# Two-layer sequence model on one core: the third token block of the feed-forward layer is turned by transfers and VectorE, and its products move past the first branches of the recurrence

## The chip, the cores and the metric

The kernel runs on one core of a Trainium2 chip. The metric is the device time of one execution in microseconds (us); the time of a kernel is the median of its runs. TensorE (PE) multiplies matrices into PSUM; VectorE (DVE), ScalarE (ACT) and GpSimd (POOL) work on tiles; SyncE (SP) issues most transfers. Every engine runs its own instructions in a fixed order and waits on semaphores for the others.

## The reference

The input is 2 x 1024 tokens of 512 floats. Two layers follow each other; each adds an attention-like part and a feed-forward part to its input and normalizes the sum over the 512 features:

```python
x = _layernorm(x + _L0_attn_ref(x, ...))   # state-space block
x = _layernorm(x + _L0_ffn_ref(x, ...))    # one linear layer, then a rescaling of each token's row
x = _layernorm(x + _L1_attn_ref(x, ...))   # gated linear recurrence
x = _layernorm(x + _L1_ffn_ref(x, ...))    # silu(x Wg) * (x Wu), then Wd
```

The two in the middle are what the change touches:

```python
# _L0_ffn_ref
out = jnp.einsum('bln,nk->blk', x, weight) * scale      # weight is -1, 0 or 1, 512 x 512
# ... out is scaled by a function of its row's norm
# _L1_attn_ref
y = gelu(x @ w_y + b_y)
xb = x @ w_x + b_x
conv = causal convolution of xb over 4 tokens
gate_x, gate_a = sigmoid(conv @ w_ig + b_ig), sigmoid(conv @ w_ag + b_ag)
h_t = a_t * h_{t-1} + x_t                                # along the tokens
out = (h * y) @ w_out + b_out
```

## The kernel before, in words

The 2048 tokens are four blocks of 512 (`NBLK`, numbered 0 to 3). A block in "row" form has tokens on the partitions (`X[b]`, four groups of 128 tokens, j = 0 to 3); a product needs it "turned", with features on the partitions (four groups of 128 features, k = 0 to 3).

The kernel has two ways to turn a block. `transposed` lets TensorE multiply by an identity, 16 products of 128 x 128, and ScalarE and VectorE take the results from PSUM. `load_blocks` and `turn_blocks` need the rows in device memory: four transfers read them so that 32 x 32 pieces come to the right place, and VectorE turns the pieces in four instructions, one for each k.

`linear(b)` is the feed-forward part of the first layer for one block. It is a generator that the code around it advances from `yield` to `yield`. Its first step turns the block and cuts it into two pieces of reduced precision: ScalarE casts the value to the high piece (tile `wu`) and VectorE subtracts that from the value for the low piece (tile `wd`). The next two steps are the products, two token groups each (`po`, 8 matmuls for a group, high and low piece by turns), each followed on VectorE by a multiplication from PSUM (`o`) and on ScalarE by a sum of squares. The last step rescales the rows, adds them to `X[b]`, normalizes (for blocks 1 to 3 the four passes of the normalization run on GpSimd), and stores the block to `x_lin`. The tiles of the two pieces have one buffer: block b+1 can be cast only when the products of block b are done.

`branches(b)` starts the recurrence for a block: four products with `w_x` (m = 0 to 3), each taken out of PSUM by ScalarE into `xpad`, a tile of two buffers with three pad columns in front, and convolved by VectorE in four instructions (one scaled copy into `cv`, three taps); then four products with `w_y`, each through GELU on ScalarE. For block 0 the pad columns are zeroed by GpSimd. `gates(b)` multiplies the convolved block by `w_ig` and `w_ag`; `project_back(b)` multiplies by `w_out` at the end.

`weave(main, fill, plan)` walks through `main` and advances `fill` by `plan[i]` steps after step i; what is left of `fill` is run at the end. A scheduler then chooses each engine's order from the program's order and its own estimates; `tc.keep_in_program_order` and `tc.high_priority` bind or raise single instructions.

Around the change the order is this. `linear(0)` and `linear(1)` run among the last products of the first layer's attention part. Then `branches(0)` is woven with `linear(2)` by the plan `(1,) * 4`: block 2 is turned by TensorE right after block 0, and its products stand between those of `w_x`. Block 3 was read in pieces (`mid`, by `load_blocks` from `x_mid`, the output of the attention part), VectorE turns it, and its products stand between those of `gates(0)`. The weights `w_out` take the buffer of the turned block 0 (tag `w4`); they are asked for in `linear(3)`.

Of the kernel before, what the change touches and what calls it, by code (L numbers as in the profile page):

```python
# [9 lines left out]
F32 = mybir.dt.float32  # L10
# [6 lines left out]
P = 128  # L17
TB = 512
NJ = TB // P
D = 512  # L20
NK = D // P
# [16 lines left out]
def model_kernel(ctx: ExitStack, tc: tile.TileContext, t: dict, out: bass.AP):  # L38
    nc = tc.nc
    ctx.enter_context(nc.allow_non_contiguous_dma(reason="small parameter columns"))  # L40
    BATCH, SEQ, _ = t["L0_attn_hidden_states"].shape
    NBLK = BATCH * SEQ // TB
# [3 lines left out]
    x_mid = tc.dram_tile([NBLK, TB, D], F32, name="x_mid")  # L46
# [35 lines left out]
    X = [tokens() for _ in range(3)]  # L82
# [49 lines left out]
    w_out = op.tile([P, NX, D], F32, tag="w_out", name="w_out")  # L132
# [90 lines left out]
        nc.vector.tensor_scalar(r, z, 0.0, None, ALU.max)  # L223
        nc.vector.scalar_tensor_tensor(o, p, 2.0, r, ALU.mult, ALU.add)

    def transposed(pool, b, X, tags=("xT",), split=False, bufs=1, by_act=False, behind=False, soon=False):


        pieces = [
            pool.tile([P, NK, TB], F32R if split else F32, tag=tag, name=f"{tag}{b}", bufs=bufs)  # L230
            for tag in tags
        ]
        xT = pieces[0]
        for k in range(NK):
            pt = bank("pt")
            for j in range(NJ):
                nc.tensor.transpose(  # L237
                    pt[:, j * P : (j + 1) * P], X[b][:, j, k * P : (k + 1) * P], ident
                )
            if split:  # L240
                copied = nc.scalar.copy(xT[:, k, :], pt)
                if behind:
                    tc.keep_in_program_order(copied)
                nc.vector.tensor_tensor(
                    pieces[1][:, k, :], pt, xT[:, k, :].bitcast(F32), ALU.subtract
                )
            elif soon:
                with tc.high_priority():
                    nc.scalar.copy(xT[:, k, :], pt)
            elif k % 2 or by_act:  # L250
                nc.scalar.copy(xT[:, k, :], pt)
            else:
                nc.vector.tensor_copy(xT[:, k, :], pt)
        return pieces
# [6 lines left out]
    def load_blocks(dst, rows, pinned=False):  # L261

        blocks = rows.rearrange("(n t) (k a c) -> a t k n c", t=32, k=NK, c=32)
        for a in range(4):
            load = nc.sync.dma_start(
                dst[32 * a : 32 * a + 32].rearrange("t k (n c) -> t k n c", c=32), blocks[a]
            )
            if pinned:
                tc.keep_in_program_order(load)

    def turn_blocks(dst, src=None, pinned=False):
        for k in range(NK):
            turned = nc.vector.transpose(dst[:, k, :], (src or dst)[:, k, :])
            if pinned:
                tc.keep_in_program_order(turned)
# [28 lines left out]
    def weave(main, fill, plan, rest=True):  # L304

        for i, _ in enumerate(main):
            for _ in range(plan[i] if i < len(plan) else 0):
                next(fill, None)
        for _ in fill if rest else ():
            pass  # L310
# [561 lines left out]
    def later_layers(exact, last=None):  # L872
# [65 lines left out]
        def split(x, pieces):  # L938


            for k in range(NK):
                nc.scalar.copy(pieces[0][:, k, :], x[:, k, :])
                if exact:
                    nc.vector.tensor_tensor(
                        pieces[1][:, k, :], x[:, k, :], pieces[0][:, k, :].bitcast(F32),
                        ALU.subtract,
                    )
# [7 lines left out]
        def linear(b):  # L955

            tags = ("wu0", "wd0") if exact else ("wu0",)
            if b == NBLK - 1:
                turn_blocks(mid)
                w1.append(wp.tile([P, NK, D], F32, tag="w4", name="w14" + suffix))  # L960
                xT = [ep.tile([P, NK, TB], WT, tag=tag, name=f"{tag}{b}") for tag in tags]
                split(mid, xT)
                nc.sync.dma_start(w1[4], w_sources["w_out"])
            else:

                xT = transposed(ep, b, X, tags=tags, split=exact, behind=b == 2)
            yield
            o = ep.tile([P, NJ, D], F32, tag="wF", name="o" + suffix)
            ssq = sp.tile([P, NJ], F32, tag="ssq", name="ssq")
            for j in range(NJ):  # L970
                po = bank("po")
                for k in range(NK):
                    for x in xT:
                        nc.tensor.matmul(  # L974
                            po, x[:, k, j * P : (j + 1) * P], wf[:, k, :],
                            start=(k == 0 and x is xT[0]), stop=(k == NK - 1 and x is xT[-1]),
                        )
                nc.vector.tensor_tensor(o[:, j, :], po, f0s, ALU.mult)
                junk = ep.tile([P, GW], mybir.dt.bfloat16, tag="junk", name="junk2")
                nc.scalar.activation(junk, o[:, j, :], AF.Square, accum_out=ssq[:, j : j + 1])  # L980
                if j % 2:
                    yield
            norm = sp.tile([P, NJ], F32, tag="norm", name="norm")
            nc.scalar.activation(norm, ssq, AF.Sqrt)
            v = sp.tile([P, NJ], F32, tag="v", name="v")
            nc.vector.tensor_scalar(v, norm, 1e-7, None, ALU.max)
            f = sp.tile([P, NJ], F32, tag="f", name="f")
            nc.scalar.activation(f, v, AF.Tanh)
            nc.vector.tensor_scalar(v, v, 1e-7, None, ALU.add)
            nc.vector.reciprocal(v, v)  # L990
            nc.vector.tensor_tensor(f, f, v, ALU.mult)
            nc.vector.tensor_tensor(norm, norm, f, ALU.mult)
            nc.vector.tensor_scalar(norm, norm, 1e-7, None, ALU.max)
            nc.vector.reciprocal(norm, norm)
            nc.vector.tensor_scalar(norm, norm, 0.99, 1.0, ALU.mult, ALU.min)
            nc.vector.tensor_tensor(f, f, norm, ALU.mult)
            for j in range(NJ):
                nc.vector.scalar_tensor_tensor(
                    X[b][:, j, :], o[:, j, :], f[:, j : j + 1], X[b][:, j, :],
                    ALU.mult, ALU.add,  # L1000
                )
            layernorm(X[b], engine=nc.gpsimd, last=None if b else nc.vector)
            if b:
                store_rows(x_lin[b], X[b])
            yield
# [39 lines left out]
        with tc.tile_pool(name="rec" + suffix, bufs=1, side="right", reuse_waits="tile") as rp:  # L1045
            carry = rp.tile([P, NK, 3], F32, tag="carry", name="carry1")
            last_h = rp.tile([P, NK], F32, tag="last", name="last")

            mid = rp.tile([P, NK, TB], F32, tag="xT", name="mid" + suffix)
            load_blocks(mid, x_mid[3])  # L1050
            nc.sync.dma_start(X[3], rows_mid[3])

            def product(i, m, rhs):
# [8 lines left out]
            def branches(b, st):  # L1062

                if b:
                    xT = rp.tile([P, NK, TB], F32, tag="xT", name=f"xT{b}")
                    turn_blocks(xT, lin.pop(0))
                    if b + 1 < NBLK:
                        lin.append(coming_block(b + 1))
                else:

                    xT = transposed(wp, b, X, tags=("w4",), by_act=True, soon=True)[0]
                yield
                cv = st["cv"] = rp.tile([P, NK, TB], F32, tag="cv", name="cv", bufs=2)
                y = st["y"] = rp.tile([P, NK, TB], F32, tag="y", name="y", bufs=2)
                for m in range(NK):
                    pm = product(0, m, xT)
                    xpad = rp.tile([P, 3 + TB], F32, tag="xpad", name="xpad1", bufs=2)
                    if b % BPS == 0:
                        nc.gpsimd.memset(xpad[:, 0:3], 0.0)
                    else:  # L1080
                        nc.gpsimd.tensor_copy(xpad[:, 0:3], carry[:, m, :])
                    nc.scalar.activation(xpad[:, 3:], pm, AF.Identity, bias=bx[:, m : m + 1])
                    if b % BPS < BPS - 1:
                        nc.gpsimd.tensor_copy(carry[:, m, :], xpad[:, TB : TB + 3])
                    nc.vector.tensor_scalar(
                        cv[:, m, :], xpad[:, 3:], cw1[:, m, 3:4], cb1[:, m : m + 1],
                        ALU.mult, ALU.add,
                    )
                    causal_conv(cv[:, m, :], xpad, cw1[:, m, :])
                    yield  # L1090
                for m in range(NK):
                    pm = product(1, m, xT)
                    nc.scalar.activation(y[:, m, :], pm, AF.Gelu, bias=by[:, m : m + 1])
                    yield
# [76 lines left out]
                yield  # L1171

            st = {}
            weave(branches(0, st), linear(2), (1,) * 4)
            lin = [coming_block(1)]
            bout = row("L1_attn_b_out", D, c1, nc.sync, "scale")
            ys = []
# [256 lines left out]
```

## Time and profile before

| what | value |
|---|---|
| median of 3 runs | 1119.91 us (1119.85 to 1121.25) |
| the profiled execution's own time | 1119.75 us |
| its span in the profile | 1118.0 us |
| TensorE busy | 1099.4 us, 98% of the span |
| VectorE busy | 704.4 us, 63% |
| ScalarE busy | 452.7 us, 40% |
| GpSimd busy | 364.5 us, 33% |

The profile is of one execution; 1.75 us of its own time lie around the span. Lines such as L237 are lines of the kernel before. A matmul of plain 32-bit floats has two records in the profile, one of the reduced 32-bit type (`fp32r`, used by `linear`) and a transposition by TensorE have one. Durations of neighbouring records overlap, so a pace is read from the starts.

### The profile page before, as it was taken

What the parts mean: (1) busy time and instruction counts of PE and PEld (TensorE: products, weight loads), DVE (VectorE), ACT (ScalarE), POOL (GpSimd) and SP (SyncE); (2) the same over time, 40 slices, a digit from 0 to 9 for tenths busy, and PEclk for the clock granted to TensorE, in tenths of its full rate; (3) what the DMA queues carried; (4) which work ended last, traced back from release to release, by engine and by line L of the source; (5) the groups of instructions that cost most, each with busy time, mean ns of one, the idle gap of its engine ahead of it and who ended that gap; (6) DMA issues with size and microseconds to landing.
All of it is one profiled execution on the core that took longest, in us unless ns stands there. A gap on an engine that the chain in (4) does not pass through costs nothing.

```text
span 1118.0 us, 12076 instructions
## 1 busy us (share of the span) xinstructions
PE 1099.4 (98%) x4450; PEld 663.6 (59%) x4450; DVE 704.4 (63%) x1267; ACT 452.7 (40%) x692; POOL 364.5 (33%) x346
## 2 busy tenths in 40 slices
PE   9999999999999999999999999999999999999996
PEld 5455445445544555745444444447888888888885
DVE  5989797697869676874647438184238865325224
ACT  3334633463454233466654372553233224224223
POOL 1546471465248340273533231236411001001000
PEclk9999999999999999999999999999999999999998
DMA  8004202801220138336550001204654002100001
GB/s 323 21 9 122 94 1 92 207 0 38 88 98 0 39 124 226 67 94 153 111 76 25 13 1 44 32 0 138 192 95 76 1 1 62 15 1 32 6 1 41
DMA packets 122059, 77.04 MB, mean 69 GB/s; under 512 B 94512, under 2 KB 95312, under 8 KB 120456
## 3 DMA queue, kind: packets, MB, share of 16 engines
q1 hardware_dynamic: 120792, 75.77, 25.6%
q8 instruction: 37, 0.61, 0.2%
q10 hardware_dynamic: 976, 0.39, 0.1%
q14 instruction: 30, 0.25, 0.1%
q0 software_dynamic: 224, 0.02, 0.0%
HBM read 59.95 MB, written 16.02 MB: 68 GB/s over the span
## 4 chain that ended last, share of the span: by engine, by line
PE 81%; DVE 11%; ACT 4%; issue 1%; POOL 1%; DMA 1%; SPq 0%; DVEq 0%; ACTq 0%; POOLq 0%
PE pgu L1026 20%; PE p L1056 19%; PE po L1257 10%; PE pg L372 9%; PE px L372 7%; PE po L770 4%; DVE acc L298 3%; PE po L1146 2%; PE py L705 2%; PE po L974 2%; DVE L L578 2%; PE pxt L674 1%; PE pt L237 1%; DVE st L283 1%; POOL x L1152 1%
## 5 line engine op out<-in xcount | busy, mean ns | idle before, releaser
L1037 DVE SCALAR_TENSOR_TENSOR h<-pgu,L_ffn_up_scale,sg 128x512 f32<-128x512 f32 x63 | 47.1, 748 | 126.6 <-PE pgu L1026 122.8
L770 PE MATMUL po<-w_out,xc 128*128 128x512 f32 x256 | 112.5, 593 | 2.8 <-DVE L L578 2.8
L372 PE MATMUL px<-xT,w_in 128*128 128x512 f32 x256 | 114.6, 597 | 0.0
L593 POOL TENSOR_TENSOR L<-L,gm 128x512 f32<-128x512 f32 x64 | 93.4, 1490 | 64.8 <-DVE bdec L588 38.3
L372 PE MATMUL pg<-xT,w_in 128*128 128x512 f32 x256 | 113.5, 594 | 0.0
L1056 PE MATMUL p<-cv,w 128*128 128x512 f32 x256 | 110.8, 592 | 0.0
L1026 PE MATMUL pgu<-wF__4239,wg 128*128 128x512 f32 x256 | 101.7, 397 | 0.0
L1026 PE MATMUL pgu<-lo__4240,wg 128*128 128x512 f32 x256 | 100.8, 394 | 0.0
L1026 PE MATMUL pgu<-lo__4240,wu 128*128 128x512 f32 x256 | 100.7, 393 | 0.0
L1026 PE MATMUL pgu<-wF__4239,wu 128*128 128x512 f32 x256 | 100.7, 393 | 0.0
L1257 PE MATMUL po<-wd,hh 128*128 128x512 f32 x252 | 98.2, 396 | 0.3 <-POOL wg L917 0.3
L1257 PE MATMUL po<-wd,hl 128*128 128x512 f32 x252 | 98.2, 396 | 0.2 <-DVE hl L1041 0.2
L1036 ACT ACTIVATE sg<-pgu,L_ffn_gate_scale 128x512 f32<-128x512 f32 x63 | 43.4, 688 | 127.7 <-PE pgu L1026 127.6
L770 PEld LDWEIGHTS po<-w_out,xc 128*128 128x128 f32 x256 | 48.4, 190 | 63.8 <-issue 56.2
L1040 ACT CAST hh<-h 128x512 fp32r<-128x512 f32 x63 | 39.1, 620 | 112.5 <-DVE h L1037 112.3
L1056 PEld LDWEIGHTS p<-cv,w 128*128 128x128 f32 x256 | 48.6, 190 | 60.4 <-issue 59.1
L1056 PE MATMUL p<-xT,w 128*128 128x512 f32 x192 | 82.9, 592 | 0.0
L372 PEld LDWEIGHTS px<-xT,w_in 128*128 128x128 f32 x256 | 47.5, 190 | 57.5 <-issue 56.0
L372 PEld LDWEIGHTS pg<-xT,w_in 128*128 128x128 f32 x256 | 47.3, 190 | 54.2 <-issue 53.3
L1375 POOL TENSOR_TENSOR x<-x,r 128x512 f32<-128x512 f32 x12 | 15.1, 1291 | 195.2 <-DVE r L1374 195.2
L298 DVE SCALAR_TENSOR_TENSOR acc<-xpad,cols,acc 128x512 f32<-128x512 f32 x72 | 67.0, 933 | 18.5 <-ACT acc L342 13.8
L578 DVE TENSOR_TENSOR_SCAN L<-pl,id 128x512 f32<-128x512 f32 x64 | 74.9, 1205 | 4.5 <-ACT pl L572 3.5
(294 smaller groups left out, 1926.1 us busy)
## 6 DMA issues: line engine op xcount, KB each, us to landing
L<-decays SPq DMA_DIRECT2D x12, 1024.0 KB, 7.3
x_mid<-x SPq DMA_DIRECT2D x4, 1024.0 KB, 4.3
x<-x_mid SPq DMA_DIRECT2D x4, 1024.0 KB, 7.9
st<-in_L_ffn_gate_w_dram SPq DMA_DIRECT2D x8, 512.0 KB, 5.8
st<-in_L_ffn_up_w_dram SPq DMA_DIRECT2D x8, 512.0 KB, 4.1
st<-in_L_ffn_down_w_dram SPq DMA_DIRECT2D x8, 512.0 KB, 3.7
x_rec<-x SPq DMA_DIRECT2D x4, 1024.0 KB, 4.7
x<-_attn_hidden_states_dram SPq DMA_DIRECT2D x3, 1024.0 KB
```

Of the source, the lines that this page charges most:

```text
L298: tap = nc.vector.scalar_tensor_tensor(acc, xpad[:, k : k + TB], w[:, k : k + 1], acc, ALU.mult, ALU.add)
L372: nc.tensor.matmul(pm[:n, :], w_in[:, k, lo : lo + n], xT[:, k, :], start=(k == 0), stop=(k == NK - 1),)
L578: nc.vector.tensor_tensor_scan(L[:, h, :], pl, id4.rearrange("p j t -> p (j t)"), 0.0, ALU.mult, ALU.add)
L593: nc.gpsimd.tensor_tensor(L[:, h, :], L[:, h, :], st["gm"], ALU.mult)
L705: nc.tensor.matmul(pys[i][hh * HD : (hh + 1) * HD, q, :], dtx[q][:, 2 * i + hh, :], L[:, h, s], start=(first and q == 0), stop=(q == 1), s ...
L770: nc.tensor.matmul(po, xc[:, m, j * P : (j + 1) * P], w_out[:, m, :], start=(m == 0), stop=(m == NX - 1),)
L1026: nc.tensor.matmul(pm, w[g][:, k, cols], x[:, k, :], start=(k == 0 and x is pieces[0]), stop=(k == NK - 1 and x is pieces[-1]),)
L1036: nc.scalar.activation(sg, pgu[0], AF.Silu, scale=gs[:, m : m + 1])
L1037: nc.vector.scalar_tensor_tensor(h, pgu[1], us[:, m : m + 1], sg, ALU.mult, ALU.mult)
L1040: nc.scalar.copy(halves[0], h)
L1056: nc.tensor.matmul(pm, w1[i][:, k, m * P : (m + 1) * P], rhs[:, k, :], start=(k == 0), stop=(k == NK - 1),)
L1257: nc.tensor.matmul(po[j], x[:, j * P : (j + 1) * P], wd[m // GK][:, m % GK, :], start=(m == 0 and x is h[0]), stop=(m == NF - 1 and x is h ...
```

## The change

Block 2 is now read in pieces and turned by VectorE as block 3 was. Both tiles are allocated at the start of the recurrence's pool, block 2 in one of the two buffers of `y`, and their eight transfers are issued with raised priority. The plan of the weave becomes `(0, 0, 0, 0, 1, 0, 1, 1)`: block 2 is turned and cut after the four products of `w_x`, its first two product groups come after the second product of `w_y`, the other two after the third, and its last step after `branches(0)`. The load of `w_out` moves from `linear(3)` to the end of that weave. The argument `behind` of `transposed`, which bound block 2's copies, goes.

```diff
-    def transposed(pool, b, X, tags=("xT",), split=False, bufs=1, by_act=False, behind=False, soon=False):
+    def transposed(pool, b, X, tags=("xT",), split=False, bufs=1, by_act=False, soon=False):
...
             if split:
-                copied = nc.scalar.copy(xT[:, k, :], pt)
-                if behind:
-                    tc.keep_in_program_order(copied)
+                nc.scalar.copy(xT[:, k, :], pt)
...
-            if b == NBLK - 1:
-                turn_blocks(mid)
-                w1.append(wp.tile([P, NK, D], F32, tag="w4", name="w14" + suffix))
+            if b > 1:
+                turn_blocks(mid[b])
                 xT = [ep.tile([P, NK, TB], WT, tag=tag, name=f"{tag}{b}") for tag in tags]
-                split(mid, xT)
-                nc.sync.dma_start(w1[4], w_sources["w_out"])
+                split(mid[b], xT)
             else:
-
-                xT = transposed(ep, b, X, tags=tags, split=exact, behind=b == 2)
+                xT = transposed(ep, b, X, tags=tags, split=exact)
...
-            mid = rp.tile([P, NK, TB], F32, tag="xT", name="mid" + suffix)
-            load_blocks(mid, x_mid[3])
+            mid = {}
+            for b, tag, bufs in ((2, "y", 2), (3, "xT", 1)):
+                mid[b] = rp.tile([P, NK, TB], F32, tag=tag, name=f"mid{b}{suffix}", bufs=bufs)
+                with tc.high_priority():
+                    load_blocks(mid[b], x_mid[b])
             nc.sync.dma_start(X[3], rows_mid[3])
...
-            weave(branches(0, st), linear(2), (1,) * 4)
+            weave(branches(0, st), linear(2), (0, 0, 0, 0, 1, 0, 1, 1))
+            w1.append(wp.tile([P, NK, D], F32, tag="w4", name="w14" + suffix))
+            nc.sync.dma_start(w1[4], w_sources["w_out"])
```

## The prediction

> **What bounds the kernel now.** I read the page's busy times first, then its chain, then the chain and each engine's timeline between 440 and 530 us, where the change lies, and last the busy times by stage at the end of the span for the clock.
>
> ```profile
> PE 1099.4 (98%) x4450; PEld 663.6 (59%) x4450; DVE 704.4 (63%) x1267; ACT 452.7 (40%) x692; POOL 364.5 (33%) x346
> PE 81%; DVE 11%; ACT 4%; issue 1%; POOL 1%; DMA 1%; SPq 0%; DVEq 0%; ACTq 0%; POOLq 0%
> ```
>
> TensorE is never far from busy: 18.6 us of 1118.0 are idle. So a change is worth the TensorE work that it takes away, less every new pause of TensorE. The chain through the stage shows that there is no pause now:
>
> ```profile
> 458.43 3.49 PE pt L237 x32
> 461.92 3.44 PE p L1056 x8
> 465.36 3.67 PE po L974 x16
> 469.03 3.43 PE p L1056 x8
> 472.46 3.64 PE po L974 x16
> 476.11 27.47 PE p L1056 x64
> ```
>
> Columns are start, length, engine and line. First come the 32 transpositions (16 of block 0, 16 of block 2), then w_x and block 2's products by turns, then w_x, w_y and the first gate products. Paces: a transposition 3.49/32 = 0.109 us; a record of p 27.47/64 = 0.429 us, so a product of four matmuls (8 records) 3.43 us; a matmul of linear 3.64/16 = 0.228 us.
>
> **What goes.** Sixteen transpositions on TensorE: 16 x 0.109 = 1.75 us, all of it on the path. That is the whole possible gain, 0.16% of the time, less than the 0.2% that a measurement of this kernel can tell from no change.
>
> **What moves on TensorE.** In the changed kernel's order of instructions TensorE runs block 0's 16 transpositions, then six products without a break (four of w_x, two of w_y), and then needs block 2's pieces. It gets there at 458.43 + 1.75 + 6 x 3.43 = 480.8 us. Nothing independent stands behind: only one matmul of w_y is put between the first of block 2's.
>
> **When the pieces are there.** On VectorE the order puts all convolutions of block 0 first, then the four turnings of block 3, then the four of block 2, then block 2's four subtractions. (Block 3's stand first although they are needed later.) The last convolution is the one that waits, for GpSimd. These are GpSimd's and VectorE's timelines of before, and one cast of ScalarE:
>
> ```profile
> 475.36 0.10 POOL L1079 MEMSET xpad<- 128x3 f32 x1 [1.40 <-DVE cv L298]
> 476.08 8.95 POOL L291 TENSOR_SCALAR x<-x,mv,rs 128x512 f32<-128x512 f32 x4 [0.62 <-DVE rs L289]
> 484.98 0.10 POOL L1079 MEMSET xpad<- 128x3 f32 x1
> ```
> ```profile
> 475.75 0.17 DVE L289 RECIPROCAL rs<-rs 128x4 f32<-128x4 f32 x1
> 490.74 0.72 DVE L298 SCALAR_TENSOR_TENSOR cv<-xpad,cw,cv 128x512 f32<-128x512 f32 x1
> 491.50 1.54 DVE L298 SCALAR_TENSOR_TENSOR cv<-xpad,cw,cv 128x512 f32<-128x512 f32 x2
> 493.04 2.46 DVE L273 STREAM_TRANSPOSE mid<-mid 128x512 f32<-128x512 f32 x4
> 495.42 0.68 DVE L944 TENSOR_TENSOR wd<-mid,wu 128x512 fp32r<-128x512 f32 x1
> ```
> ```profile
> 493.75 0.62 ACT L942 CAST wu<-mid 128x512 fp32r<-128x512 f32 x1 [1.58 <-DVE mid L273]
> ```
>
> The fourth xpad's pad columns are zeroed (484.98) behind the four normalization passes of block 1, since GpSimd keeps its order; that order is the same after the change, and the first tap reads those columns. Before, this cost nothing: VectorE was late itself (first tap 490.74) and TensorE asked for the convolved block only after 496. Now TensorE's next products stand behind it. Step by step:
>
> - Start of the passes. VectorE loses four subtractions of block 2 (L244) and two multiplications (L978) ahead of it, and its first convolution starts about 2 us earlier, because TensorE delivers w_x's first product at 460.2 + 3.4 = 463.6 instead of 465.4. But one tap more (0.67) comes before the last statistics, and ScalarE takes out the third product (0.6) before the table load and the square root. I put the passes at 475.3 instead of 476.1; bounds 474.8 and 476.1.
> - Their length. Block 1's four took 8.95 us, beside a VectorE that was busy throughout; block 3's took 8.24 at 530.08. VectorE will be idle for the second half, so 8.7. Pads zeroed at 484.1 (bounds 483.1 to 485.1).
> - Three taps: from 490.74 to 492.95 with an aggregate between them, so 2.1. Done at 486.2.
> - Block 3's four turnings: 495.42 - 493.04 = 2.38, done at 488.6. Block 2's first cast can start 0.71 after its first turning (493.75 - 493.04) and takes 0.62; with 0.1 for the semaphore TensorE resumes at 490.0.
> - The subtractions wait for all eight turnings: 486.2 + 4.76 = 491.0, then four at 0.62 give 493.5. The last matmul of the first token group ends at 493.7.
>
> From 480.8 to 493.7 TensorE has nine matmuls of linear (2.05 us) and one of w_y (0.86): 2.9 us of work in 12.9. The pause is 10.0 us, and from there on TensorE has everything.
>
> **The clock.** A pause this long has a second price. At the end of the span the last matmul is over by 1109; these are the busy times by stage, with the granted clock third from the end:
>
> ```profile
> 1108.00:1110.00 2.00, 0.88 (x4) 0.38 (x2) 1.93 (x6) 1.62 (x5) 1.28 (x2) 1.00 0.28 93
> 1110.00:1112.00 2.00, 0.00 (x0) 0.00 (x0) 1.58 (x4) 1.94 (x6) 0.13 (x1) 0.88 0.46 166
> 1112.00:1114.00 2.00, 0.00 (x0) 0.00 (x0) 0.71 (x2) 0.14 (x1) 0.00 (x0) 0.50 0.52 186
> ```
>
> After some 2.6 us without matmuls the clock is 0.50. How long it stays there once work is back, no row shows directly; the nearest is the span's start, where 24 records of 128 x 128 (L188) take 4.92 us, 0.205 each, twice the 0.107 that 0.429 for 512 columns would make. Bounds: nothing, or 4.92 us at half speed from 490.0. In the second case 2.46 us of the 2.9 are done at 494.9, and the group ends at 495.35 instead of 493.7, 1.65 us lost. I take the middle, 0.85.
>
> [...]
>
> **What costs nothing, and its cover.** SP issues eight loads of 256 KB (1.15 us each by its timeline: 3 in 3.45) instead of four, from 462 on, all ahead of block 1's store to x_lin, which waits for GpSimd until 484 anyway. Before, three were in by about 470; eight are in by 480 at the latest, six us before the turning at 486. Without that cover each us late is a us lost. The load of w_out now waits for the last w_y product, at about 505, on SP's queue; the last quarter of block 1's lin load (needed after 515) stands behind it. It lands some 7 us after its issue, so at 512; cover 3 us and more. VectorE gains four turnings (2.4 us) and loses nothing else; it sits in the pause. Block 3's casts wait for block 2's last product, now 3.43 + 2 x 3.43 = 10.3 us ahead of block 3's first product (27 us before). Behind four casts (2.2), a table load (1.28) and a sum of squares (0.8) that is enough.
>
> **Sum.** -1.75 + 10.0 + 0.85 = +9.1 us on the profiled 1119.75, so 1128.9; the median of the runs stands 0.16 above that execution: 1129.0.
>
> **Rivals.**
> - Faster: the pieces are ready before TensorE asks, and only the 16 transpositions go: 1119.9 - 1.75 = 1118.2. It needs VectorE to begin the eight turnings by 473.5 (480.8 less 7.3 for turnings and subtractions). Against it stands the order: at 475.75 VectorE was still at block 1's statistics. Three chances in 100.
> - GpSimd isn't in the way (the tap does not wait for the zeroed pads). Then VectorE's own work counts: the fourth convolution starts about 478.5, done 480.6, last subtraction 487.9, pause 488.1 - 480.8 - 2.9 = 4.4. With 0.5 for the clock: +3.2, 1123.1. For it: the row 476.08 names only rs as its releaser. Against: taps read the pad columns. Eight in 100.
> - A second pause: block 3's pieces come late as well, the 10.3 us being too few for ScalarE's queue of casts, table loads and GELUs. Two to four us more: 1132.0. For it: block 1's pieces were 0.8 us late at 451.74 in the same form. Seven in 100.
>
> **How the numbers follow.** The forecast has 82 in 100. Its own bounds: pads 483.1 to 485.1 (-1.0, +1.0) and the clock 0 to 1.65 (-0.85, +0.8) give 1127.1 to 1130.8. I stretch that to 1126.0 and 1132.0, which takes in most of the second pause and leaves out the other two rivals. Faster by over 0.2% (under 1117.7): 0.02, the first rival's far end. Same: 0.02. Slower: 0.96.
>
> **What would show it.** Right: TensorE's records stop near 481 and resume near 490, at the first po of L974, with a granted clock of 0.50 there; block 2's turnings on VectorE lie after a tap that GpSimd's memset released; 80 records of L237 instead of 96. Wrong: no pause at L974, or one that ends on a transfer of mid. If VectorE's first tap of the fourth xpad runs before the passes on GpSimd end, the second rival has it.

## Result and profile after

| | before | changed |
|---|---|---|
| median | 1119.91 us | 1131.39 us (1129.75 to 1132.53) |
| the profiled execution's own time | 1119.75 us | 1129.75 us |
| its span | 1118.0 us | 1128.0 us |

The ratio to the kernel before is 1.0096, interval 1.0083 to 1.0108. The change costs 11.5 us by the medians and 10.0 us between the two profiled executions. In the changed kernel the turnings are L271, the normalization passes L289, the taps L296, casts and subtractions L940 and L942, `linear` L969, the products of the branches L1054 and the zeroing of the pads L1077.

The page's busy times hardly move; TensorE does the same work with 16 instructions fewer:

```profile
PE 1099.6 (97%) x4434; PEld 662.7 (59%) x4434; DVE 709.6 (63%) x1271; ACT 451.7 (40%) x691; POOL 365.3 (32%) x346
PE 78%; DVE 12%; ACT 4%; issue 2%; POOL 2%; DMA 1%; SPq 0%; DVEq 0%; ACTq 0%; POOLq 0%
```

The second line is the chain: three points of it have gone from TensorE to others. TensorE's timeline shows where (start, length, engine, line, and in brackets the idle time ahead with its releaser):

```profile
458.16 1.91 PE L237 MATMUL pt<-ident,x 128*128 128x128 f32 x16
459.90 20.77 PE L1054 MATMUL p<-w,w 128*128 128x512 f32 x48
490.83 1.22 PE L969 MATMUL po<-wfr,wu 128*128 128x512 f32 x2 [10.16 <-ACT wu L940]
...
506.69 7.03 PE L1054 MATMUL p<-cv,w 128*128 128x512 f32 x16
```
TensorE stops at 480.7, after six products, and resumes at 490.83 with block 2's first matmul; its list of waits has no other new entry of this size. The first gate product starts at 506.69, 10.15 later than before (496.54). Block 3's products (513.15) begin without a wait, so there is no second pause. Who held the pieces up is read from GpSimd, VectorE and ScalarE, in this order:

```profile
475.33 9.39 POOL L289 TENSOR_SCALAR x<-x,mv,rs 128x512 f32<-128x512 f32 x4 [1.36 <-issue]
484.66 0.10 POOL L1077 MEMSET xpad<- 128x3 f32 x1
```
```profile
478.20 0.54 DVE L1083 TENSOR_SCALAR cv<-xpad,cw,L_attn_conv_b 128x512 f32<-128x512 f32 x1
484.80 2.34 DVE L296 SCALAR_TENSOR_TENSOR cv<-xpad,cw,cv 128x512 f32<-128x512 f32 x3 [6.05 <-POOL xpad L1077]
487.05 4.86 DVE L271 STREAM_TRANSPOSE mid<-mid 128x512 f32<-128x512 f32 x8
491.83 2.45 DVE L942 TENSOR_TENSOR wd<-mid,wu 128x512 fp32r<-128x512 f32 x4
```
```profile
490.16 2.40 ACT L940 CAST wu<-mid 128x512 fp32r<-128x512 f32 x4 [8.77 <-DVE mid L271]
```

VectorE stands still for 6 us in front of a tap that needs three zeroed columns from GpSimd. GpSimd zeroes them only after four normalization passes of block 1. The eight turnings, the casts and the subtractions that TensorE needs all stand behind that tap.

### The profile page after: what moved, and what is told of

Its sections match the earlier page's. It is cut to its first block, busy times and chain, and to the rows that moved or that the text cites. A ratio compares the mean times of both kernels' runs of the same rounds, so it can differ in the third digit from the quotient of the medians.

```text
span 1128.0 us, 12048 instructions
## 1 busy us (share of the span) xinstructions
PE 1099.6 (97%) x4434; PEld 662.7 (59%) x4434; DVE 709.6 (63%) x1271; ACT 451.7 (40%) x691; POOL 365.3 (32%) x346
## 4 chain that ended last, share of the span: by engine, by line
PE 78%; DVE 12%; ACT 4%; issue 2%; POOL 2%; DMA 1%; SPq 0%; DVEq 0%; ACTq 0%; POOLq 0%
PE pgu L1021 20%; PE p L1054 17%; PE po L1257 10%; PE pg L370 9%; PE px L370 7%; PE po L768 4%; DVE acc L296 3%; PE po L1144 2%; PE py L703 2%; DVE L L576 2%; PE po L969 2%; PE pxt L672 1%; DVE st L281 1%; POOL x L1150 1%; PE py L695 1%
## 5 line engine op out<-in xcount | busy, mean ns | idle before, releaser
L1054 PE MATMUL p<-cv,w 128*128 128x512 f32 x256 | 110.8, 592 | 0.0
L1054 PEld LDWEIGHTS p<-cv,w 128*128 128x128 f32 x256 | 48.6, 190 | 60.4 <-issue 58.6
L1054 PE MATMUL p<-xT,w 128*128 128x512 f32 x192 | 82.9, 592 | 0.0
L296 DVE SCALAR_TENSOR_TENSOR acc<-xpad,cols,acc 128x512 f32<-128x512 f32 x72 | 67.1, 933 | 18.5 <-ACT acc L340 13.8
```

The source lines that it names most:

```text
L296: tap = nc.vector.scalar_tensor_tensor(acc, xpad[:, k : k + TB], w[:, k : k + 1], acc, ALU.mult, ALU.add)
L1054: nc.tensor.matmul(pm, w1[i][:, k, m * P : (m + 1) * P], rhs[:, k, :], start=(k == 0), stop=(k == NK - 1),)
```

## Experiments

Whole times carry a disturbance from elsewhere: in some executions (four of the ten profiled) the clock drops to 0.50 for 3.4 us near 143 us, far ahead of the change (last section). In the profiles that show it, it moves this stage by 1.0 to 1.5 us. So beside the medians I give the length of the stage, from the first transposition of block 0 to the first gate product, which doesn't contain it. For before it is 496.54 - 458.27 = 38.27 us, for the changed kernel 506.69 - 458.16 = 48.53. Ratios are to the kernel before (median 1120.48 beside the first four, 1120.26 beside the others).

**The pads zeroed by VectorE.**

```diff
                     if b % BPS == 0:
-                        nc.gpsimd.memset(xpad[:, 0:3], 0.0)
+                        (nc.gpsimd if b else nc.vector).memset(xpad[:, 0:3], 0.0)
```

> The changed kernel, but the pad columns of block 0's four xpads are zeroed by VectorE, so that no tap waits for GpSimd's passes of block 1. GpSimd as the gate (the prediction's theory): the last block's first tap runs at about 478.5 instead of 484.8, the eight turnings end at about 485.7, TensorE resumes at about 484.6 and its pause is 3.9 instead of 10.2 us, too short for the clock to stay low for long; with the clock's 0.9 back, 5 to 7 us less than the changed kernel's 1131.4: 1124.0 to 1126.5. VectorE's own queue as the gate: the turnings stay where they are and the time stays at 1131 within 1. Late transfers of the pieces: nothing moves either, and the first turning waits for a DMA.

Measured: 1125.3 us, ratio 1.0041 (1.0028 to 1.0055). VectorE's and TensorE's timelines:

```profile
479.68 2.72 DVE L296 SCALAR_TENSOR_TENSOR cv<-xpad,cw,cv 128x512 f32<-128x512 f32 x3
482.31 4.86 DVE L271 STREAM_TRANSPOSE mid<-mid 128x512 f32<-128x512 f32 x8
```
```profile
486.10 1.22 PE L969 MATMUL po<-wfr,wu 128*128 128x512 f32 x2 [4.31 <-ACT wu L940]
```

Four zeroings of three columns each, moved to another engine, take 6 us off the loss and nearly 6 off the pause (10.16 to 4.31). VectorE runs through its taps without an idle gap; GpSimd's passes still end at 486.5 in this execution, and nobody waits for them. So GpSimd's order was the gate. The rest of the pause is VectorE's own queue, in which turnings and subtractions come last. The stage takes 43.71 us, 5.44 over before: -1.75 for the transpositions, +4.31 for the pause and 2.9 for what the pause does to the clock and to the first matmuls, which this run doesn't separate. I had expected the clock to stay low for a shorter time here; it stayed low for 5.4 us after work was back, longer than in the changed kernel's profile.

**The products later.**

```diff
-            weave(branches(0, st), linear(2), (0, 0, 0, 0, 1, 0, 1, 1))
+            weave(branches(0, st), linear(2), (0, 0, 0, 0, 1))
```

> The changed kernel, with block 2's products behind all four products of w_y instead of two: TensorE has two products (6.9 us) more to do while the pieces are made; everything else keeps its order. If the pause is only work that is missing while the pieces are late (the prediction's theory), it shrinks from 10.2 to about 3.2 us and resumption stays at 490.8; with the clock not cold for long, 1123 to 1125. If something that follows TensorE sets the pieces (banks, ScalarE behind the GELUs), resumption moves too, to 495 and more, and the time stays at 1129 or above.

Measured: 1126.01 us, ratio 1.0042 (1.0027 to 1.0058).

```profile
491.90 2.07 PE L969 MATMUL po<-wfr,wu 128*128 128x512 f32 x4 [3.29 <-ACT wu L940]
```

The pause is 3.29 us, as expected (3.2), and resumption did not move: this execution's stage starts 1.08 later than the changed kernel's, and so does resumption (491.90 against 490.83). The pieces come when they come, and TensorE's missing work is all that makes the pause. The time missed its forecast (up to 1125) by 1 us. The stage is 42.83, that is 38.27 - 1.75 + 3.29 + 3.0. The last term is the price of the clock, which stayed at half for 5.9 us after the pause, together with any wait for the subtractions; this run doesn't separate the two. In the changed kernel both together are 48.53 - 38.27 + 1.75 - 10.16 = 1.85, so a pause two thirds shorter did not make this part cheaper.

**Block 2 on TensorE again, in the new place.**

```diff
-            for b, tag, bufs in ((2, "y", 2), (3, "xT", 1)):
+            for b, tag, bufs in ((3, "xT", 1),):
...
-            if b > 1:
+            if b == NBLK - 1:
                 turn_blocks(mid[b])
```

> The changed kernel, but block 2 is turned by TensorE again (16 transpositions, the pieces taken from the bank, no load of its copy); the place of its products is the new one, behind two products of w_y. If the pause came from the transfers and turnings of block 2, it goes, and the time is that of before, 1120 within 1. If the place of the products behind convolutions that wait for GpSimd is enough, VectorE's subtractions of block 2 stand behind the tap that waits until 484.8, TensorE waits some 2 to 3.5 us at wd, and the time is 1122 to 1124: two thirds of the loss would then belong to the turnings behind that tap, and one third to the place.

Measured: 1126.37 us, ratio 1.0049 (1.0034 to 1.0065); stage 43.37.

```profile
486.40 0.76 DVE L296 SCALAR_TENSOR_TENSOR cv<-xpad,cw,cv 128x512 f32<-128x512 f32 x1 [5.38 <-POOL xpad L1077]
487.09 0.68 DVE L242 TENSOR_TENSOR wd<-pt,wu 128x512 fp32r<-128x512 f32 x1
```
```profile
487.82 0.80 PE L969 MATMUL po<-wfr,wd 128*128 128x512 f32 x1 [3.10 <-DVE wd L242]
```

The stage alone is 5.1 us longer than before, though nothing of block 2 is transferred or turned by VectorE. Two of its subtractions are now queued behind the tap that waits for GpSimd; 3.1 us are TensorE's wait for the first of them, 2.0 come after it, at half clock (0.50 until 491.1) and with subtractions and taps by turns. The mechanism was as expected, and my range (up to 1124) was too low, as I had no price for the second part. So the new place alone, with TensorE turning, loses about half of what the whole change does.

**Turned early, in the order of the program.** Computation and engines are those of the changed kernel; what differs is the weave's plan and who orders VectorE and ScalarE.

```diff
-            weave(branches(0, st), linear(2), (0, 0, 0, 0, 1, 0, 1, 1))
+            with tc.manual_schedule(
+                engines={mybir.EngineType.DVE, mybir.EngineType.Activation}
+            ):
+                weave(branches(0, st), linear(2), (0, 0, 1, 0, 0, 0, 0, 1, 1))
```

> The changed kernel with VectorE's and ScalarE's instructions of this stage kept in the order in which the program writes them, and the steps written so that block 2's turnings, casts and subtractions come after the second convolution of block 0 and its products after the third product of w_y. The same instructions on the same engines as in the changed kernel. If order alone made the pause, it is gone: TensorE runs through, only the 16 transpositions are missing, and the time is 1.75 under before, 1118.2 (1117.7 to 1119.0). If transfers, bank turnover or VectorE's load are a cost of their own, a pause of 1 us or more stays at the first product of block 2 or of block 3 and the time is 1119.5 or above.

Measured: 1117.94 us, ratio 0.9981 (0.9972 to 0.9990): faster than both kernels. The chain between 455 and 520 us is TensorE alone:

```profile
458.45 1.75 PE pt L237 x16
460.20 24.04 PE p L1054 x56
484.24 0.47 PE po L969 x2
484.71 0.86 PE p L1054 x2
485.56 3.20 PE po L969 x14
```

VectorE turns the blocks before the third and fourth convolution; GpSimd zeroes the last pads at 483.68, and the fourth convolution needs them only at 489.3:

```profile
479.22 4.87 DVE L271 STREAM_TRANSPOSE mid<-mid 128x512 f32<-128x512 f32 x8 [3.61 <-DMA mid<-x_mid]
484.01 2.45 DVE L942 TENSOR_TENSOR wd<-mid,wu 128x512 fp32r<-128x512 f32 x4
```

The stage takes 36.54 us, 1.73 under before, where 16 x 0.109 = 1.75 was the whole possible gain. So the transfers and the turnings cost nothing where they are early enough, and the 12.0 us between this stage and the changed kernel's are the price of the order. TensorE's order is part of it: the new plan gives it one product more, 3.4 us, before it asks for block 2 (484.24 instead of 480.7). How much the orders of VectorE and ScalarE bring without that was not measured. The bracket shows the next limit: VectorE has waited for the transfers since 475.6. The turnings can't begin before 479.2, so the pieces are ready (first cast done at 482.9) only 1.3 us before TensorE asks. The first cast starts at 482.34, when five of the eight turnings are done: block 3's four, which are needed later, still come first and take 2.4 us. Whether block 2's could begin as early in their place was not tried.

**The changed kernel again, and with the clock kept up.** Ten products of weights by weights, into a bank that nobody reads, fill most of the pause:

```diff
             yield
+            if b == 2 and exact:
+                warm = bank("warm")
+                for _ in range(10):
+                    nc.tensor.matmul(warm, w1[1][:, 0, :P], w1[1][:, 0, :], start=True, stop=True)
             o = ep.tile([P, NJ, D], F32, tag="wF", name="o" + suffix)
```

> The changed kernel once more, as the base for the next run on the same chip: 1131.4 within 1, a pause of 10.2 us, and a stretch at half clock behind it that lasts 3 to 6 us in the profiled execution.

> The changed kernel with ten products more on TensorE ahead of block 2's (weights by weights, 0.86 us each, into a bank that nobody reads), so that it works through 8.6 us of the pause and waits only the last 1.5. Resumption is set by ScalarE's cast and stays at 490.8. The prediction's clock term (0.85 of the loss): the first token group of block 2 runs at a granted clock of 1.00, paced by VectorE's subtractions until 494.4, and the time is 0.9 less than the changed kernel's, 1130.5. If the cold stretch is mostly longer than in the profiled execution of the changed kernel (3.2 us; 5.4 and 5.9 in the first two experiments), its price is up to 2.9: 1128.5 to 1129.5, and the runs scatter less. If the clock costs nothing because the subtractions pace TensorE anyway, the time stays at 1131.4.

Measured: 1131.32 us again (1.0099, 1.0083 to 1.0114), and 1130.65 with the clock kept (1.0087, 1.0073 to 1.0101). Busy times by stage, the granted clock third from the end, first of the changed kernel again and then with the products:

```profile
489.00:491.00 2.00, 0.13 (x1) 0.13 (x1) 2.00 (x4) 0.80 (x2) 0.00 (x0) 0.50 0.85 283
493.00:495.00 2.00, 2.00 (x5) 1.19 (x5) 1.33 (x3) 0.00 (x0) 0.00 (x0) 0.50 1.10 140
```
```profile
489.00:491.00 2.00, 0.49 (x2) 0.00 (x0) 2.00 (x5) 0.61 (x2) 0.00 (x0) 1.00 0.92 250
493.00:495.00 2.00, 2.00 (x8) 1.05 (x8) 1.51 (x3) 0.00 (x0) 0.00 (x0) 1.00 1.08 146
```

The medians differ by 0.7, but their intervals overlap. The stages give the clock's price more closely, because resumption lies equally far from the stage's start in all three (32.7 us): 47.77 with the clock kept, 48.53 in the first profile of the changed kernel, 49.68 in the second. So the clock costs 0.76 in one execution and 1.91 in another.

**ScalarE's order left to the scheduler.** As turned early, without `Activation` among the ordered engines.

> As the experiment with the turnings early, but ScalarE's order is left as in the changed kernel: the casts of block 2 stand behind the GELU of the third w_y product, which waits for TensorE. So TensorE waits about 1.5 us at the first product of block 2 (one GELU and one cast, 0.7 + 0.6, behind its own last product). VectorE's order as the larger part (the theory): 1119.4 to 1120.0, that is 10 of the 12 us come back by VectorE's order alone and 1.5 by ScalarE's. If a pause of 1.5 us is enough for the clock to fall, 1 to 2 more: 1121 to 1122. If ScalarE's order mattered as much as VectorE's, over 1123.

Measured: 1120.27 us, ratio 0.9998 (0.9989 to 1.0008), 0.3 above the range expected.

```profile
485.44 0.72 PE L969 MATMUL po<-wfr,wu 128*128 128x512 f32 x2 [1.28 <-ACT wu L940]
```

The stage is 38.10, 1.56 over that with both orders. VectorE's order with the new plan gives back 10.4 of the 12.0 us, ScalarE's the rest: one cast behind one GELU is enough to use up the gain of the change. The clock stays at 1.00 through this pause (every row from 480 to 490 us). (GpSimd's order, which neither version binds, came out differently too: here it zeroes the last pads at 475.65, ahead of its passes. The fourth convolution comes at 490.7, so nothing waits for them in either.)

**The old place.**

```diff
-            weave(branches(0, st), linear(2), (0, 0, 0, 0, 1, 0, 1, 1))
+            weave(branches(0, st), linear(2), (1,) * 4)
```

> The changed kernel with block 2's products in their old place, by turns with the products of w_x, so block 2 is turned by transfers and VectorE but nothing is moved. Block 2's turnings stand after block 3's and behind block 1's statistics on VectorE: TensorE does one product of w_x and waits from 463.6 to about 480.6, 17 us, and the time is 1120 - 1.75 + 17 + 1 to 2 for the clock = 1136 to 1138. If the new place were what costs, the time would be under the changed kernel's 1131.

Measured: 1140.09 us, ratio 1.0172 (1.0157 to 1.0188), 2 us above the range expected.

```profile
480.50 4.87 DVE L271 STREAM_TRANSPOSE mid<-mid 128x512 f32<-128x512 f32 x8 [4.36 <-DMA mid<-x_mid]
```
```profile
484.29 1.22 PE L969 MATMUL po<-wfr,wu 128*128 128x512 f32 x2 [19.16 <-ACT wu L940]
```

So the products had to move once block 2 comes by transfers. The pause is 19.2 and not 17, as here the transfers are late and not GpSimd: VectorE is free at 476 and waits for them until 480.5. I had taken its turnings to be held by its own queue.

## Why the prediction was right

The mechanism is the one predicted, and each step of it stands in the lines above: the pause before the first po, the tap released by GpSimd's memset, the turnings behind that tap, a clock of 0.50 (in the rows of the second profile). Moving four memsets took the pause from 10.2 to 4.3 us. The terms, predicted against measured:

- Transpositions: -1.75; the version without a pause gained 1.73 in the stage.
- Start of GpSimd's passes: 475.3; measured 475.33. Their length: 8.7; measured 9.39, outside the bounds of 8.24 to 8.95. The argument was that an idle VectorE would let them run at their best for half of the time. In the old place, where VectorE was idle or turning, all four passes took 2072 ns; in the changed kernel, beside taps, the longest took 2940, and it was one of the first two: the chain has the last two start at 480.59 and take 4.13 together, beside an idle VectorE. So 3.6 us of taps at the start cost more than I gave for half of the time. (The wait alone was in range: pads at 484.66, bounds 483.1 to 485.1.)
- Taps: 2.1, measured 2.25; turnings, casts and subtractions each followed within 0.1 of their lengths. The 0.1 put in for the semaphore between cast and product was an estimate; by the chain the first cast is done at 490.79, 0.04 before the product. So TensorE resumed at 490.83 instead of 490.0, with a pause of 10.16 instead of 9.2.
- Pace behind the subtractions: 12.9 less 9.2 of pause and 2.9 of work, that is 0.8; measured 1.09. In the stage with the clock kept, TensorE needs 5.45 us from resumption to the next product of w_y, and 4.36 where the pieces are early.
- Clock: 0.85; measured 0.76 in the profiled execution and 1.91 in the other one. The bound of 1.65 was too low, because it stopped at the first 4.92 us of half speed; 5.4 to 5.9 us occur.

Together: -1.75 + 10.16 + 1.09 + 0.76 = 10.26, just what the stage grew by (48.53 - 38.27), against 9.1 predicted. (The 10.0 that the prediction calls the pause contain the 0.8 of pace.) The median stands 1.6 above the profiled execution, not 0.16: its cold stretch was the shorter of the two profiled, and the disturbance near 143 us was not in it. So some luck is in the range that held: 1131.39 lies above the forecast's own bounds (1127.1 to 1130.8). It is inside the range only because that was stretched to 1132.0 for a second pause, which did not come; by the profiles, longer GpSimd passes, a price of the clock above its bound and the disturbance took up that room instead.

The covers held. SP needed 1.65 us for each of eight loads (13.21 in all), not 1.15, but the DMA engines are done with them at 478.9, near the 480 of the prediction, and the turnings start at 487. With early turnings it is different: in the version turned early and in the old place VectorE waits for these transfers, until 479.2 and 480.5. So the first rival was impossible for a second reason, which the prediction didn't see: with the loads issued as they are, turnings at 473.5 were excluded by the transfers, whatever VectorE's order.

Of the rivals, the one in which GpSimd is not in the way is the first experiment. Its 4.4 us contained some 0.8 of pace, so about 3.6 of pause; measured are 4.31. The time is 1125.3 instead of its 1123.1, as the pause is 0.7 longer and clock and pace together took 2.9 instead of 1.3. A second pause did not come.

## What to carry to other kernels

When work leaves the bounding engine for one that keeps a queue, look up what stands at that queue's head at the moment of need, and whom that waits for: here three columns on a third engine decided 6 us, and the same instructions in another order turned a loss of 10 us in this stage into a gain of 1.7. Count the gain of such a change as an upper limit, the pause as work missing while the pieces are late, and add to a pause of the matmul engine of 3.1 us or more, which lowered the clock to 0.50 in all six profiles here that have one, a price that can differ from one execution to the next (here 0.76 and 1.91 us for the same pause).

## What the runs showed of the hardware

In the seven stretches below, the clock was low for 3.4 us or a multiple of that, within 0.1. The rows below are of the first experiment near 143 us, the clock third from the end: a pause of 1.95 us (140.46 to 142.41) is over, work is back, and only then, at about 143.4, the clock falls to 0.50, until 146.8.

```profile
142.00:143.00 1.00, 0.59 (x2) 0.35 (x3) 1.00 (x2) 1.00 (x3) 0.00 (x0) 1.00 0.00 0
143.00:144.00 1.00, 1.00 (x3) 0.46 (x2) 0.97 (x3) 0.39 (x1) 0.00 (x0) 0.68 0.00 0
144.00:146.00 2.00, 2.00 (x4) 0.73 (x3) 2.00 (x3) 0.00 (x0) 1.99 (x2) 0.50 0.00 0
146.00:147.00 1.00, 1.00 (x3) 0.46 (x2) 1.00 (x2) 0.00 (x0) 1.00 (x2) 0.61 0.00 0
```

In rows of 0.25 and 0.5 us the clock is 1.00 or 0.50, save for one row at each change. So a row that is 0.68 on average is taken to be at 1.00 for 36% and at 0.50 for the rest, which gives the instants. Worked out in this way:

| stretch | pause | from the last matmul to the fall | from work's return to full speed | low in all |
|---|---|---|---|---|
| changed | 10.16 | 3.2 | 3.2 | 10.2 |
| changed again | 10.16 | 2.3 | 5.8 | 13.7 |
| pads by VectorE | 4.31 | 2.9 | 5.4 | 6.8 |
| products later | 3.29 | 2.4 | 5.9 | 6.8 |
| block 2 on TensorE | 3.10 | 2.9 | 3.2 | 3.4 |
| old place | 19.16 | 2.8 | 4.2 | 20.5 |
| pads by VectorE, at 141 us | 1.95 | 2.9 | 4.4 | 3.4 |

The last column is 1, 2, 3, 4 and 6 times 3.4, within 0.1. No run shows what sets this length. The price follows the length: the same pause of 10.16 came with 10.2 us of low clock and a cost of 0.76 in one execution, and with 13.7 and 1.91 in the other. Nor do the runs show how long a pause must be for the clock to fall: one of 1.95 us was enough in four of the ten executions profiled, though not in the kernel before (1.00 throughout from 140 to 147 us, after the same pause of 1.95); one of 1.28 did nothing in the one execution profiled.

GpSimd's pass over 128 x 512 took 2072 ns with VectorE idle or turning (old place, first line: shortest, median and longest of four), up to 2940 beside taps in the changed kernel (second line), and up to 3737 ns for a single one beside VectorE's taps and copies in the first experiment. In the old place the last two of the four passes ran beside turnings (from 480.5) and took 2072 like the first two.

```profile
L289 POOL TENSOR_SCALAR x<-x,mv,rs x4: 2072/2072/2072, 476.3 to 482.5; 128x512 f32<-128x512 f32 x4
L289 POOL TENSOR_SCALAR x<-x,mv,rs x4: 2072/2212/2940, 475.3 to 482.6; 128x512 f32<-128x512 f32 x4
```
